# Four graph-attention layers: normalised rows transposed by DMA, and a changed opening

## The chip, the cores and the metric

The kernel runs on one core of one Trainium2 chip. The metric is the device time of one execution in microseconds (us), lower being better; the number given for a kernel is the median of several executions.

## The reference

The input is `x` with 16 batches of 1024 nodes and 256 features, and an adjacency matrix of 1024 x 1024. Four layers follow each other, each with a residual connection:

```python
h = jnp.maximum(_layernorm(x, axis=-1), 0.0)
x = x + layer(h, adj, W, a)
```

A layer projects the rows (`Wh = h @ W`), forms for each pair of nodes i, j a score `leaky_relu(e_src[i] + e_dst[j])`, masks it by the adjacency matrix, takes the softmax over j, sums the projected rows with these weights and applies elu (the last layer: relu). Layers 0 and 2 have four heads of 64 features, layers 1 and 3 one head of 256.

## The kernel before, in words

One step is one layer of one batch; there are 64 steps. Four batches (streams) are in work at a time, and `order_of_steps` interleaves them so that, from step 7 to step 58, four-head and one-head steps alternate. At the start three four-head steps follow each other, and near the end (steps 59 and 60) two.

The 1024 nodes lie as 8 chunks of 128 partitions. The work of a step falls into three parts.

**Preparation** (`preparation(n)`) is a list of 21 small pieces: row statistics of each half (four chunks) on VectorE (DVE, L238), their combination on GpSimd (POOL), `normalise` on ScalarE (ACT, L283), `transpose` on TensorE (PE, L291) with an eviction that applies relu (L292), `project` for each chunk on PE (L302) with its eviction to `whx` (L304), two exponentials (L310, L312), a scaling on POOL (L314), `factors`, and `rows`, which transposes the small matrix of factors (L326), copies it (L328), writes it to DRAM as `grow` (L330) and so makes it possible to fetch it back as rows. For each head `fetch` reads one row of `grow` into all partitions (`gs`, L344, on the SP queue), and `broadcast` copies it to PSUM as `g` (L350, ACT).

**Weights and aggregation.** For each head and each chunk of source nodes, `weights` makes one tile `w` of 128 x 1024 on DVE (L355). `aggregate` multiplies these with `whx` on PE (L371), in eight groups per step: in a four-head step two groups per head, each over four chunks of target nodes; in a one-head step one group per chunk. ACT copies each result out of PSUM to `y` (L386). A head's eight `w` tiles are used by all its groups, and come free after the last one. The ring of `w` tiles has `WBUFS = 18` buffers. PSUM banks for PE's results are a ring of four.

**Finish** (`finish(n)`), during the next step: reciprocal (L403), scaling (L413 on DVE or L416 on POOL, L414 on POOL), exponential (L420), and the additions for elu and residual (L426, L427; L429 in the last layer).

The order is written by hand. Each kind of step has a table (`FOUR`, `SHORT`, `ONE`, `SOON`, `FIRST`, `TIGHT`, `LATE`) with 21 due times, one per piece of the preparation in the order: two statistics, combination, two normalisations, two transposes of the first half, four projections, two transposes of the second half, four projections, factors, rows, fetch, end. The unit is a group, the zero is the start of step n - 2, and eight units are a step. After the aggregation of group k of step n the kernel emits all pieces that are due by 8 n + k. The first step's pieces are ordered by a list of their own, `order`, between the pieces that build the two masks (`sign`, `turn` on PE, `positive` on DVE L211, `nonzero`, the squares, on ACT L215). Every engine works through its instructions in the order in which they were emitted, and so does SP with its transfers.

Of the kernel before, what the change touches and what calls it, by code (L numbers as in the profile page):

```python
# [26 lines left out]
F32 = mybir.dt.float32  # L27
BF16 = mybir.dt.bfloat16
I32 = mybir.dt.int32
U8 = mybir.dt.uint8  # L30
AF = mybir.ActivationFunctionType
ALU = mybir.AluOpType
AX = mybir.AxisListType
# [2 lines left out]
P = 128  # L36
EPS = 1e-5
SHIFT = 60.0
STREAMS = 4
WBUFS = 18  # L40

# [1 line left out]

FOUR = (-8, -8, -5, -3, -2, -1, -1, 0, 0, 0, 0, 0, 0, 2, 2, 2, 2, 3, 8, 8, 10)
SHORT = (-4, -4, -4, -2, -2, -1, -1, 0, 0, 0, 0, 0, 0, 2, 2, 2, 2, 3, 8, 8, 10)
ONE = (2, 2, 2, 4, 4, 5, 5, 6, 6, 6, 6, 6, 6, 8, 8, 8, 8, 8, 10, 10, 12)  # L50
SOON = (0, 0, 0, 1, 2, 3, 3, 4, 4, 5, 5, 5, 5, 6, 6, 7, 7, 8, 9, 9, 11)
FIRST = (-4, -4, -4, -2, 0, -1, -1, -1, -1, -1, -1, 1, 1, 2, 2, 2, 2, 2, 3, 3, 5)
TIGHT = (5, 5, 5, 7, 7, 8, 8, 9, 9, 9, 9, 9, 9, 10, 10, 10, 10, 10, 11, 11, 13)
LATE = (0, 0, 0, 1, 1, 2, 2, 3, 3, 3, 3, 3, 3, 4, 4, 4, 4, 5, 6, 6, 8)


LAYERS = [
    (4, 0.2, 0, 0),
    (1, 0.2, 0, 0),
    (4, 0.2, 128, 1),  # L60
    (1, 0.01, 0, 1),
]
# [3 lines left out]
def kernel(ctx: ExitStack, tc: tile.TileContext, x, adj, ws, avs, out):  # L66
    nc = tc.nc
    B, N, F = x.shape
    C = N // P
    K = F // P  # L70
# [155 lines left out]
    def preparation(n):  # L226
# [50 lines left out]
            engine.tensor_scalar(shift, shift, -0.5, None, op0=ALU.mult)  # L277

        def normalise(half):
            xn = st["xn", half] = prep.tile([P, HALF, F], F32, name="xn")  # L280
            for q in range(HALF):
                c = half * HALF + q
                nc.scalar.activation(xn[:, q, :], xs[b][:, c, :], AF.Identity,  # L283
                                     bias=st["shift"][:, c:c + 1], scale=st["rstd"][:, c:c + 1])

        def transpose(half, k):
            if k == 0:
                st["hT", half] = prep.tile([P, K, HALF * P], F32, name="hT")
            pt = bank(HALF, P)
            for q in range(HALF):  # L290
                nc.tensor.transpose(pt[:, q, :], st["xn", half][:, q, k * P:(k + 1) * P], ident)  # L291
            nc.scalar.activation(st["hT", half][:, k, :], pt.rearrange("p q i -> p (q i)"),  # L292
                                 AF.Relu)

        def project(c):
            if c == 0:
# [43 lines left out]

    def fetch(n, h):

        gs = state[n]["gs", h] = work.tile([P, N], F32, name="gs", bufs=2)
        nc.sync.dma_start(out=gs, in_=state[n]["grow"][h].rearrange("c i -> (c i)")  # L344
                          .partition_broadcast(P))

    def broadcast(n, h):

        g = state[n]["g", h] = ps_g.tile([P, N], F32, name="g")
        nc.scalar.activation(g, state[n]["gs", h], AF.Copy)  # L350

    def weights(n, h, jc):
# [6 lines left out]
    def aggregate(n, h, i0, per):  # L359
# [25 lines left out]
            return  # L385
        nc.scalar.activation(st["y"][:, i0:i0 + per, h, :], acc, AF.Copy)  # L386

    def finish(n):

        b, l = steps[n]  # L390
        H = LAYERS[l][0]
        D = F // H
        st = state[n]

        def views(half):
            s = slice(half * HALF, (half + 1) * HALF)
            return (xs[b][:, s, :].rearrange("p c (h d) -> p (c h) d", h=H),
                    st["y"][:, s, :, 0:D].rearrange("p c h d -> p (c h) d"),
                    st["r"][:, s, :].rearrange("p c h -> p (c h)"))

        def divide():
            st["r"] = small.tile([P, C, H], F32, name="r")
            nc.vector.reciprocal(st["r"], st["y"][:, :, :, D])  # L403

        def scaled(half):
            xh, yh, r = views(half)
            rb = r[:, :, None].to_broadcast([P, HALF * H, D])
            time = LAYERS[steps[n + 1][1]][0] == 1
            if l < L - 1:

                e = st["e", half] = prep.tile([P, HALF * H, D], F32, name="e")
                if time:
                    nc.vector.scalar_tensor_tensor(e, yh, 0.0, rb, op0=ALU.min, op1=ALU.mult)  # L413
            nc.gpsimd.tensor_tensor(yh, yh, rb, op=ALU.mult)  # L414
            if l < L - 1 and not time:
                nc.gpsimd.tensor_scalar(e, yh, 0.0, -3.0e38, op0=ALU.min, op1=ALU.max)  # L416

        def exponential(half):
            if l < L - 1:
                nc.scalar.activation(st["e", half], st["e", half], AF.Exp)  # L420

        def add(half):
            xh, yh, r = views(half)
            if l < L - 1:
                e = st["e", half]
                nc.vector.scalar_tensor_tensor(e, e, -1.0, yh, op0=ALU.add, op1=ALU.max)  # L426
                nc.gpsimd.tensor_add(xh, xh, e)  # L427
                return
            nc.vector.scalar_tensor_tensor(xh, yh, 0.0, xh, op0=ALU.max, op1=ALU.add)  # L429

        def store(half):
            nc.sync.dma_start(
                out=out[b].rearrange("(p c) f -> p c f", p=P)[:, half * HALF:(half + 1) * HALF],
                in_=xs[b][:, half * HALF:(half + 1) * HALF, :])
            if half == 1 and b + STREAMS < B:
                load(b + STREAMS)


        at = (0, 0, 0, 0, 1, 1, 1) if H > 1 else (0, 0, 1, 1, 2, 2, 3)
        return list(zip(at, (divide, lambda: scaled(0), lambda: scaled(1), lambda: exponential(0),  # L440
                             lambda: exponential(1), lambda: add(0), lambda: add(1)))) + (
                    [(4, lambda: store(0)), (4, lambda: store(1))] if l == L - 1 else [])
# [15 lines left out]
    def prepare(upto):  # L458

        while agenda and agenda[0][0] <= upto:  # L460
            _, n, piece, last = agenda.pop(0)
            piece()
            if last:
                done["prepared"] = n + 1
# [16 lines left out]
    def emit_heads(i):  # L481

        while done["g"] <= min(i + C // 2, done["tiles"] + C, len(tiles) - 1):
            n, h, _ = tiles[done["g"]]
            if n >= done["prepared"]:
                break
            broadcast(n, h)
            done["g"] += C
            fetch_heads()

    def emit_tiles(upto, must=False):
        while done["tiles"] < min(upto, len(tiles)):
            i = done["tiles"]
            if i == done["g"] and tiles[i][0] >= done["prepared"] and must:
                prepare(max(a[0] for a in agenda if a[1] == tiles[i][0]))
            emit_heads(i)
            if i >= done["g"]:
                return
            weights(*tiles[i])
            done["tiles"] += 1  # L500

    last, agenda_of = {}, []
    for n, (b, l) in enumerate(steps):

        free = 8 * (last[b % STREAMS] + 1) + (8 if l == 0 else 2) if b % STREAMS in last else -99
        last[b % STREAMS] = n
        start = 8 * (n - 2) + (n == 3)
        kind = (ONE if n < len(steps) - 2 else TIGHT) if LAYERS[l][0] == 1 else SOON if n < 5 else FOUR
        if kind is FOUR and free > start + kind[0]:
            kind = SHORT  # L510
        if free > start + kind[0]:
            kind = LATE
            start = max(free, agenda_of[-1][0] + 5, start - LATE[7])
        agenda_of.append([start + k for k in kind] if n > 1 else FIRST)
        if n > 2:

            assert agenda_of[n][7] >= 8 * (n - 2)
            was = agenda_of[n - 1]
            assert agenda_of[n][3] >= was[5] and agenda_of[n][4] >= was[11]
    ending = []  # L520
    later = {}
    with tc.manual_schedule():
# [9 lines left out]
        for i in range(2, STREAMS):  # L532
# [10 lines left out]

            + [blocks[c][1] for c in range(4)]
            + [first[7], first[8], blocks[0][2], blocks[4][1], blocks[5][1], blocks[0][3],
               first[9], first[10], blocks[1][2], blocks[0][4], blocks[6][1], blocks[7][1],
               blocks[1][3], first[11], first[12], blocks[2][2], blocks[1][4],
               lambda: prepare(-4), first[13], first[14], blocks[3][2], blocks[2][4],
               blocks[2][3], blocks[3][3], first[15], first[16]]

            + [first[17], blocks[4][2], blocks[5][2], first[18], first[19],
               blocks[4][3], blocks[3][4], blocks[4][4], blocks[5][3], blocks[5][4],
               blocks[6][2], blocks[7][2], blocks[6][3], blocks[6][4], blocks[7][3], blocks[7][4]])
        plan(1)
        planned = 2
        for piece in order:
            piece()
        done["prepared"] = 1
        emit_tiles(C // 2, must=True)
        prepare(-2)  # L560
        emit_tiles(C, must=True)
        prepare(-1)
        for i in range(2, STREAMS):
            load_weights(i)

# [59 lines left out]
```

## Time and profile before

| | |
|---|---|
| median of 10 runs | 2562.13 us (2559.81 to 2564.59) |
| the profiled execution | 2562.18 us, of which the span is 2560.4 us |
| mean granted TensorE clock | 0.992 |
| PE busy | 2495.2 us, 97% of the span |
| DVE busy | 2019.2 us, 79% |
| ACT busy | 1130.7 us, 44% |
| POOL busy | 1112.2 us, 43% |
| DMA | 129.01 MB moved, queue q1 13.7% of 16 engines' time |

The span runs from the first to the last instruction. Busy times of PE count matmuls as overlapping stretches; PEld is the loading of the stationary operand, which overlaps with them. In a group's row the columns are the busy time, the mean duration of one instruction in ns, and the idle time of its engine just before them with what ended it.

### The profile page before, as it was taken

Reading aid. Unit: us, or ns where it says so; the run is one execution under the profiler, and the core shown is the slowest. Engines: PE = TensorE matmul, PEld = TensorE weight load, DVE = VectorE, ACT = ScalarE, POOL = GpSimd, SP = SyncE. Lnnn points to the kernel's source line nnn. Section 1 sums busy time; section 2 is a strip of 40 time slices with the busy share of each in tenths; the row PEclk is TensorE's granted clock in tenths of the full one; section 3 lists DMA queues with packets and bytes.
Section 4 is the critical chain, followed back from the end, with each engine's and each line's share of the span. In section 5 each row is a group of like instructions: output and inputs, shape, how many; then the busy total and the mean of one; then the engine's idle time right before and its main releaser. Section 6 shows DMA issues by size and latency. Waiting matters only on the chain.

```text
span 2560.4 us, 88174 instructions
## 1 busy us (share of the span) xinstructions
PE 2495.2 (97%) x40088; PEld 2256.7 (88%) x40088; DVE 2019.2 (79%) x2140; ACT 1130.7 (44%) x2502; POOL 1112.2 (43%) x1364
## 2 busy tenths in 40 slices
PE   6889999999999999999999999999999999999899
PEld 5788889999988999988899889999888899898887
DVE  8888577888778888778888778878778878778863
ACT  5344454434444444544434544444444444544331
POOL 3244455533444544544333544543443444644341
PEclk8999999999999999999999999999999999999999
DMA  5101011121211110111221111111112210111101
GB/s 182 53 27 43 10 43 35 44 77 47 73 43 68 44 44 11 43 43 68 77 75 45 43 35 44 43 41 46 72 40 76 76 36 19 43 35 43 61 10 58
DMA packets 36991, 129.01 MB, mean 50 GB/s; under 512 B 6278, under 2 KB 9094, under 8 KB 34696
## 3 DMA queue, kind: packets, MB, share of 16 engines
q1 hardware_dynamic: 36606, 123.36, 13.7%
q8 instruction: 314, 5.14, 0.8%
q14 instruction: 61, 0.50, 0.1%
q10 hardware_dynamic: 10, 0.00, 0.0%
HBM read 105.91 MB, written 17.43 MB: 48 GB/s over the span
## 4 chain that ended last, share of the span: by engine, by line
PE 88%; DVE 6%; ACT 3%; issue 2%; POOL 1%; DMA 0%; DVEq 0%; POOLq 0%; ACTq 0%
PE bank L371 68%; PE bank L302 15%; DVE w L355 5%; PE bank L291 4%; ACT xn L283 2%; DVE bn L238 0%; PE bank L326 0%; POOL y L414 0%; POOL e L416 0%; ACT g L350 0%; ACT y L386 0%; POOL shift L277 0%; DVE e L426 0%; DMA x<-in_x 0%; DMA gs<-grow 0%
## 5 line engine op out<-in xcount | busy, mean ns | idle before, releaser
L371 PE MATMUL bank<-whx,w 128*64 128x65 f32 x36864 | 1908.5, 241 | 30.9 <-DVE w L355 17.5
L371 PEld LDWEIGHTS bank<-whx,w 128*64 128x64 f32 x36864 | 1744.0, 145 | 175.8 <-DVE w L355 24.1
L355 DVE SCALAR_TENSOR_TENSOR w<-g,rcol,mask 128x1024 f32<-128x1024 f32 x1280 | 1540.3, 1273 | 392.1 <-PE bank L371 316.0
L386 ACT ACTIVATE y<-bank 128x260 f32<-128x260 f32 (+1 forms) x504 | 194.3, 385 | 1091.5 <-PE bank L371 1091.5
L414 POOL TENSOR_TENSOR y<-y,r 128x1024 f32<-128x1024 f32 x126 | 263.6, 2102 | 580.2 <-DVE e L413 448.8
L314 POOL TENSOR_TENSOR whx<-whx 128x1024 f32<-128x1024 f32 x128 | 257.8, 2014 | 581.7 <-ACT whx L312 581.7
L302 PE MATMUL bank<-wx,hT 128*128 128x264 f32 (+1 forms) x2048 | 482.1, 388 | 6.4 <-ACT y L386 4.3
L302 PEld LDWEIGHTS bank<-wx,hT 128*128 128x128 f32 x2048 | 382.5, 191 | 77.2 <-ACT y L386 15.5
L427 POOL TENSOR_TENSOR x<-x,e 128x1024 f32<-128x1024 f32 x96 | 248.0, 2594 | 136.4 <-DVE e L426 135.3
L283 ACT ACTIVATE xn<-x,shift,rstd 128x256 f32<-128x256 f32 x512 | 264.7, 590 | 73.1 <-POOL shift L277 70.6
L304 ACT ACTIVATE whx<-bank 128x264 f32<-128x264 f32 (+1 forms) x512 | 189.2, 385 | 177.9 <-PE bank L302 177.6
L238 DVE BATCH_NORM_STATS2 bn<-x 128x6 f32<-128x256 f32 x512 | 175.9, 411 | 79.6 <-POOL x L427 76.3
L426 DVE SCALAR_TENSOR_TENSOR e<-e,y 128x1024 f32<-128x1024 f32 x96 | 154.2, 1625 | 37.5 <-ACT e L420 30.3
L350 ACT ACTIVATE g<-gs 128x1024 f32<-128x1024 f32 x160 | 163.5, 1022 | 11.4 <-DVE w L355 9.7
L291 PE MATMUL bank<-ident,xn 128*128 128x128 f32 x1024 | 137.0, 276 | 10.4 <-ACT xn L283 10.2
L291 PEld LDWEIGHTS bank<-ident,xn 128*128 128x128 f32 x1024 | 120.1, 142 | 27.6 <-ACT xn L283 14.5
L292 ACT ACTIVATE hT<-bank 128x512 f32<-128x512 f32 x256 | 136.9, 586 | 1.3 <-PE bank L291 1.0
L271 POOL TENSOR_TENSOR rstd<-rstd,neghalf 128x4 f32<-128x4 f32 (+1 forms) x97 | 120.4, 1241 | 15.1 <-DVE shift L272 7.7
L420 ACT ACTIVATE e<-e 128x1024 f32<-128x1024 f32 x96 | 100.7, 1049 | 24.2 <-POOL e L416 23.8
L413 DVE SCALAR_TENSOR_TENSOR e<-y,r 128x1024 f32<-128x1024 f32 x60 | 72.5, 1250 | 2.2
L429 DVE SCALAR_TENSOR_TENSOR x<-y,x 128x1024 f32<-128x1024 f32 x30 | 44.9, 1499 | 2.0 <-POOL y L414 2.0
L265 POOL TENSOR_TENSOR dev<-bn 128x4 f32<-128x4 f32 (+1 forms) x95 | 20.7, 217 | 49.3 <-DVE bn L238 49.2
(63 smaller groups left out, 463.4 us busy)
## 6 DMA issues: line engine op xcount, KB each, us to landing
gs<-grow SPq DMA_DIRECT2D x160, 512.0 KB
x<-in_x SPq DMA_DIRECT2D x15, 1024.0 KB
out<-x SPq DMA_DIRECT2D x30, 512.0 KB
w<-in_adj SPq DMA_DIRECT2D x8, 512.0 KB
x<-in_x SPq DMA_DIRECT2D x2, 512.0 KB
wx<-in_L_gnn_W SPq DMA_DIRECT2D x8, 128.0 KB
out<-x SPq DMA_DIRECT2D x8, 128.0 KB
grow<-gT SPq DMA_DIRECT2D x32, 16.0 KB
```

The source lines that it names most:

```text
L238: nc.vector.bn_stats(bn[:, c, :], xs[b][:, c, :])
L283: nc.scalar.activation(xn[:, q, :], xs[b][:, c, :], AF.Identity, bias=st["shift"][:, c:c + 1], scale=st["rstd"][:, c:c + 1])
L291: nc.tensor.transpose(pt[:, q, :], st["xn", half][:, q, k * P:(k + 1) * P], ident)
L302: nc.tensor.matmul(pw, lhsT=st["hT", half][:, k, q * P:(q + 1) * P], rhs=wx[l][:, k, :], start=(k == 0), stop=(k == K - 1))
L304: nc.scalar.activation(st["whx"][:, c, :], pw, AF.Copy)
L314: nc.gpsimd.tensor_tensor(wh[:, :, :, 0:D], wh[:, :, :, 0:D], wh[:, :, :, D:D + 1].to_broadcast([P, HALF, H, D]), op=ALU.mult)
L350: nc.scalar.activation(g, state[n]["gs", h], AF.Copy)
L355: nc.vector.scalar_tensor_tensor(w, state[n]["g", h], state[n]["rcol"][:, jc, h:h + 1], masks[LAYERS[steps[n][1]][3]][:, jc, :], op0=ALU.m ...
L371: nc.tensor.matmul(acc[o % P:o % P + cols, q, :], lhsT=st["w", h, jc][:, o:o + cols], rhs=st["whx"][:, jc, h * (D + 1):(h + 1) * (D + 1)], ...
L386: nc.scalar.activation(st["y"][:, i0:i0 + per, h, :], acc, AF.Copy)
L414: nc.gpsimd.tensor_tensor(yh, yh, rb, op=ALU.mult)
L427: nc.gpsimd.tensor_add(xh, xh, e)
```

## The change

The core of the diff, in two parts. The first part alters the opening. For head 0 of step 0, `fetch` does nothing and `broadcast` makes `g` by eight PE transposes of the factors, each with a column spread over 128:

```diff
     def broadcast(n, h):
         g = state[n]["g", h] = ps_g.tile([P, N], F32, name="g")
+        if n == 0 and h == 0:
+            for c in range(C):
+                nc.tensor.transpose(g[:, c * P:(c + 1) * P],
+                                    state[n]["gcol"][:, c, h:h + 1].to_broadcast([P, P]), ident)
+            return
         nc.scalar.activation(g, state[n]["gs", h], AF.Copy)
```

The list `order` changes, the squares of a pair of masks standing behind both of the pair's `positive`. In `finish`, a four-head step that is followed by another four-head step spreads its pieces over groups 0 to 3; the scaling on DVE (L413) now needs four heads and a following one-head step:

```diff
+    def slack(n):
+        return LAYERS[steps[n + 1][1]][0] == 1
...
-            time = LAYERS[steps[n + 1][1]][0] == 1
...
-                if time:
+                if H > 1 and slack(n):
...
-        at = (0, 0, 0, 0, 1, 1, 1) if H > 1 else (0, 0, 1, 1, 2, 2, 3)
+        at = (0, 0, 0, 0, 1, 1, 1) if slack(n) and H > 1 else (0, 0, 1, 1, 2, 2, 3)
```

The second part concerns the transposes. From step 2 on, PE's transposes and their evictions are replaced. `normalise` applies the relu and writes its result with the two halves of the features outermost. `split` copies it on ACT as 16-bit integers, all lower halves of the words ahead of all upper halves; a transposing DMA from the SP queue turns each of the 16 blocks of 128 x 128; `merge` puts the halves together again on ACT. The two pieces of `transpose` are now `split` and `merge`:

```diff
+        def split(half):
+            xn = st["xn", half].rearrange("p k q i -> p (k q i)").bitcast(U16)
+            bits = prep.tile([P, 2, K * HALF * P], U16, name="rows", bufs=HBUFS)
+            nc.scalar.activation(bits, xn.rearrange("p (n s) -> p s n", s=2), AF.Copy)
+            st["turned", half] = prep.tile([P, 2, K * HALF, P], U16, name="rows", bufs=HBUFS)
+            nc.sync.dma_start_transpose(
+                out=st["turned", half].rearrange("p s n i -> p (s n) i"),
+                in_=bits.rearrange("p s n -> p (s n)"))
+
+        def merge(half):
+            st["hT", half] = prep.tile([P, K, HALF * P], F32, name="rows", bufs=HBUFS)
+            nc.scalar.activation(
+                st["hT", half].rearrange("p k i -> p (k i)").bitcast(U16).rearrange(
+                    "p (n s) -> p n s", s=2),
+                st["turned", half].rearrange("p s n i -> p (n i) s"), AF.Copy)
+
         def transpose(half, k):
+            if n > 1:
+                (merge if k else split)(half)
+                return
```

The buffers of `xn`, `hT` and the new tiles become one ring `rows` of `HBUFS = 5`, and `WBUFS` goes from 18 to 17. The tables get new due times; the two that the alternating steps use are

```diff
-FOUR = (-8, -8, -5, -3, -2, -1, -1, 0, 0, 0, 0, 0, 0, 2, 2, 2, 2, 3, 8, 8, 10)
+FOUR = (-8, -8, -5, 0, 2, 1, 4, 5, 5, 5, 5, 3, 4.5, 5, 5, 5, 5, 6, 8, 8, 10)
-ONE = (2, 2, 2, 4, 4, 5, 5, 6, 6, 6, 6, 6, 6, 8, 8, 8, 8, 8, 10, 10, 12)
+ONE = (2, 2, 2, 3, 4, 3, 5, 7, 7, 7, 7, 4, 7, 8, 8, 8, 8, 8, 11, 11, 12)
```

## The prediction

> **What bounds the kernel now.** I read the page from the top: busy shares first, then the chain that ended last, then the costliest groups.
>
> ```profile
> span 2560.4 us, 88174 instructions
> ...
> PE 2495.2 (97%) x40088; PEld 2256.7 (88%) x40088; DVE 2019.2 (79%) x2140; ACT 1130.7 (44%) x2502; POOL 1112.2 (43%) x1364
> ...
> PE 88%; DVE 6%; ACT 3%; issue 2%; POOL 1%; DMA 0%; DVEq 0%; POOLq 0%; ACTq 0%
> PE bank L371 68%; PE bank L302 15%; DVE w L355 5%; PE bank L291 4%; ACT xn L283 2%; DVE bn L238 0%; PE bank L326 0%; POOL y L414 0%; POOL e L416 0%; ACT g L350 0%; ACT y L386 0%; POOL shift L277 0%; DVE e L426 0%; DMA x<-in_x 0%; DMA gs<-grow 0%
> ...
> L355 DVE SCALAR_TENSOR_TENSOR w<-g,rcol,mask 128x1024 f32<-128x1024 f32 x1280 | 1540.3, 1273 | 392.1 <-PE bank L371 316.0
> ...
> L350 ACT ACTIVATE g<-gs 128x1024 f32<-128x1024 f32 x160 | 163.5, 1022 | 11.4 <-DVE w L355 9.7
> L291 PE MATMUL bank<-ident,xn 128*128 128x128 f32 x1024 | 137.0, 276 | 10.4 <-ACT xn L283 10.2
> ...
> L292 ACT ACTIVATE hT<-bank 128x512 f32<-128x512 f32 x256 | 136.9, 586 | 1.3 <-PE bank L291 1.0
> ```
>
> TensorE is busy 97% and carries 88% of the chain; 4% is L291, the transposes that the change takes away. DVE comes second and waits for PE (316 us): its w tiles are made ahead until the 18 buffers are full. Those buffers are the only cushion, so I asked the windows for one pair of steps in the middle (a four-head step at 1051.19, then a one-head step) and for the opening.
>
> ```profile
> 1051.19:1127.96 76.77, 76.68 (x1252) 69.72 (x1254) 61.49 (x65) 35.84 (x80) 38.50 (x45) 1.00 0.12 37
> ...
> 45.80:200.50 154.70, 136.94 (x3249) 126.36 (x3249) 134.17 (x138) 62.23 (x133) 50.88 (x63) 0.93 0.10 34
> ```
>
> Columns: length, then busy PE, PEld, DVE, ACT, POOL, clock, DMA share, GB/s. In the pair PE has no hole (76.68 of 76.77) and DVE has 15 us to spare. In the opening, three four-head steps in a row, PE has 18 us of holes: there DVE paces. The timeline of the pair gives the unit prices:
>
> ```profile
> 1051.12 3.95 PE L371 MATMUL bank<-whx,w 128*64 128x65 f32 x128
> 1055.00 7.31 PE L302 MATMUL bank<-wx,hT 128*128 128x258 f32 x32
> 1062.15 1.04 PE L291 MATMUL bank<-ident,xn 128*128 128x128 f32 x8
> 1063.12 7.69 PE L371 MATMUL bank<-whx,w 128*64 128x65 f32 x256
> ```
>
> and DVE's own timeline of the same stretch:
>
> ```profile
> 1066.30 7.24 DVE L355 SCALAR_TENSOR_TENSOR w<-g,rcol,mask 128x1024 f32<-128x1024 f32 x6 [9.29 <-PE bank L371]
> ```
>
> From start to start, eight transposes cost 0.97 us of PE, eight projections 7.2 (0.9 each), a group of a four-head step 3.75 to 3.88; a w tile is 1.2 us of DVE. The 9.29 us in brackets is DVE waiting until PE has used up head 0.
>
> **What the Trainium skill says.** "ScalarE: Activation LUTs", section "What ACT_TABLE_LOAD costs": an activation costs a fixed part and 0.833 ns per element, float32 or bf16 alike. The trace agrees on float32, (1022 - 385) / (1024 - 260) = 0.834 ns between L350 and L386; no run here shows 16-bit elements two apart. "VectorE: DVE Perf Modes", section "The three transpose paths": 390 ns for a 128x128 bf16 transpose on TensorE and 1309 ns by the DMA crossbar. In the trace one float32 transpose is 272 ns recorded but 0.12 us in a run of eight; no DMA transpose is in it. "DMA: Bandwidth & Descriptors", section "Latency and other measured facts": 261 GB/s for DMA transposes. "Advanced Engine Details and Errata", section "X-Bar Transpose (TRN2)": they are about as fast as plain ones, and only one stream may transpose at a time; here SP alone issues them.
>
> **The change part by part**
>
> *Transposes of steps 2 to 63.* 62 steps x 2 halves = 124 halves, each with eight PE transposes: 124 x 0.98 us = 121.5 us leave PE. Steps 2, 3 and 4 are prepared in the opening, where DVE paces: 3 x 1.96 = 5.9 us bring nothing. Counted: -115.6 us.
>
> *ACT.* Per half two evictions L292 go (2 x 0.586 = 1.17 us); a split and a merge of 2048 elements come, each 1.022 + 1024 x 0.000834 = 1.88 us. So +2.58 us per half, 124 x 2.58 = +320 us: ACT goes from 1131 to about 1450 us, 59% of the new span, not a bound. Relu moves into the normalisation at no cost. Behind a split or merge wait the evictions of y and whx, and PE waits for those when its four banks are full; a group lasts 3.5 to 3.75 us, so a bank is free for over 10 us in aggregation, and a delay of 1.9 us is covered there. In a burst of projections (0.9 us each) the cover is only some 3 us: zero taken, up to +15 us kept for the range.
>
> *The DMA.* Each half sends 128 x 2048 x 2 bytes = 0.5 MB on SP's queue. The nearest row is the gs fetch of the same size: 3.92 us from issue to arrival (32.60 to 36.52 on the chain). By the skill's bandwidth, an estimate of 524288 / 261000 = 2.0 us of transfer, with the roughly 1.7 us that the gs fetch has beside its 2.2 us of issue spacing (four of them in 8.84 us in the pair's timeline): 3.7 us. By the skill's 1309 ns per block, sixteen blocks end to end: 20.9 us. I take 5 us. SP's instruction waits for the split; behind it on SP stand the gs fetches, x loads and stores, whose rows are needed a head or more later. The added 62 MB is half of what q1 moves in 13.7% of the engines' time, so about 7% more.
>
> *Is 5 us hidden?* In a four-head step the second half is split after group 3 and merged after group 5. After group 3's end ACT takes y (0.39) and the split (1.88), so the transfer has 2 x 3.75 - 2.27 = 5.2 us before ACT itself must wait. PE has four projections of the first half (3.6 us) before it needs the merge (1.88): 5.2 + 3.6 - 1.9 = 6.9 us. In a one-head step (groups of 3.47 us) the same working, with normalisation and split in one group and a first transfer before the second, also gives about 7. So 5 us cost nothing and each us beyond 7 costs PE about 1 us per step.
>
> *Projections bunched, 17 buffers.* FOUR now puts all eight projections at group 5; before, four stood at group 0 and four at group 2 of that step, and gave DVE time. So: head 0 is used up at 3.75 + 3.65 (the one-head step's four projections) + 3.75 = 11.2 us. With 17 buffers DVE has then made 16 tiles and one of head 2; seven more (8.4 us) and an elu add between (1.24) end at 20.8. PE is through head 1 at 18.7 and can use seven tiles, to 19.5. **A new wait of 1.3 us** in each of about 28 such steps: +36 us. Afterwards the eight projections (7.2 us) restore DVE's lead. Bounds: 0 (a longer group gives the time back) and 2.5 us per step, one tile more late.
>
> *The first G.* grow, gs and the copy go; eight PE transposes (1.0 us) take their place. Before, gcol is ready at 30.06, G at 37.56, and DVE ends its masks at 34.49; now masks bound: 37.60 - 34.49 = -3.1 us. The other order of first pieces, squares behind masks, prepares in the opening, and the elu spread over groups 0 to 3 where four heads follow four act on the 18 us of holes there; not priced by any row, so bounded by 0 and -15; I take -9. Together -12.
>
> Sum: -115.6 + 36 - 12 = -92 us against the profiled execution's 2562.18 (span 2560.4 and 1.8 around it), which equals the median, 2562.13. **Forecast 2470 us.**
>
> **Rivals**
>
> *Part of the gain is eaten* (2500 to 2556): the wait on w is 2.5 us per step (+34 more), or the transfer takes 7.5 us (31 us more), or ACT's burst costs its 15. For it: DVE falls from 15 to 11 us of slack per pair. Against it: the lead is regained each step.
>
> *The transfer lands late* (slower): from 7 us on, each us costs 62 us; the 92 us gained are gone at 7 + 1.5 = 8.5 us. At 10 us the time is 2470 + 3 x 62 = 2656. For it: 1309 ns per block in sequence gives 20.9, transfers of two halves queue behind each other and behind the gs fetches. Against it: the DMA engines are 12% busy, and both bandwidth figures lie far below the point. If 16-bit elements cost ACT two beats, split and merge gain 1.7 us each and eat the same window; with 5 us that ends near zero gain.
>
> *It does not do what it says*: steps 0 and 1 keep PE transposes (32 records); all others must go.
>
> **How the numbers follow.** Forecast case 0.50, by its bounds 2430 to 2500. Eaten gain 0.27. Within 0.2%, about what a measurement tells from no change, 0.04. Slower 0.19, nearly all by late landing. The range goes from 2430 (0.04 below: no wait on w and all of the opening) to 2570 (0.17 above). The likeliest sign's own range is 2430 to 2556.
>
> **What would show it.** L291 down to 32 transposes on PE; PE near 2375 us; a pair near 74.2 us (76.8 - 3.9 + 1.3); PE idle before L371 by DVE w, about 1.3 us in each four-head step; split and merge at 1.88 us; a DMA transpose under 7 us; L302 waiting for a merge nowhere. I am wrong if ACT waits long for the transposing DMA and PE's idle is put down to that, or if DVE's w waits vanish.

## The result, and the profile after

| | before | after |
|---|---|---|
| median | 2562.18 us (29 runs) | 2478.91 us (8 runs, 2476.93 to 2482.28) |
| ratio, with its 95% interval | | 0.9678 (0.9669 to 0.9686) |
| the profiled execution, and its span | 2562.18 us, 2560.4 | 2482.28 us, 2480.5 |

The change makes the kernel 83.3 us faster; 92 were forecast. These are the lines of the page after it: busy shares, queue q1, the chain that ended last, and the costliest groups. The lines have moved: L283, L291, L302, L304, L355, L371, L386 and L350 are now L285 (normalise), L316 (the transposes left on PE), L327 (project), L329 (eviction to `whx`), L388 (`w`), L404 (aggregate), L419 (eviction to `y`) and L383 (copy of `g`). New are L294 (split), L296 (the transposing DMA) and L302 (merge).

```profile
span 2480.5 us, 86492 instructions
...
PE 2404.1 (97%) x39104; PEld 2156.7 (87%) x39104; DVE 2044.5 (82%) x2138; ACT 1481.5 (60%) x2501; POOL 1073.0 (43%) x1366
...
q1 hardware_dynamic: 294382, 187.86, 30.4%
...
PE 87%; DVE 6%; DMA 3%; ACT 2%; issue 2%; POOL 1%; DVEq 0%; SPq 0%; ACTq 0%; POOLq 0%
...
L388 DVE SCALAR_TENSOR_TENSOR w<-g,rcol,mask 128x1024 f32<-128x1024 f32 x1280 | 1540.6, 1272 | 230.7 <-PE bank L404 134.4
...
L302 ACT ACTIVATE rows<-rows 128x2048 uint16<-128x2048 uint16 x124 | 265.7, 2143 | 15.8 <-DMA rows<-rows 15.8
L294 ACT ACTIVATE rows<-rows 128x2048 uint16<-128x2048 uint16 x124 | 236.2, 1904 | 2.2
...
rows<-rows SPq DMA_TRANSPOSE x124
```

PE is still the bound, and 91 of its busy microseconds are gone. ACT has 351 more. DVE waits for PE 134 us where it waited 316: its lead in `w` tiles has shrunk. In the windows, the pair of steps that is shown and the opening answer to those of before (length, busy PE, PEld, DVE, ACT, POOL, clock, DMA share, GB/s):

```profile
1019.30:1093.50 74.20, 73.97 (x1219) 66.37 (x1218) 63.17 (x65) 47.11 (x79) 36.68 (x44) 1.00 0.28 66
943.97:1019.30 75.33, 73.83 (x1219) 66.51 (x1218) 63.09 (x65) 47.10 (x79) 36.69 (x44) 1.00 0.30 65
45.30:185.40 140.10, 128.36 (x3201) 117.73 (x3201) 133.90 (x139) 77.02 (x130) 49.38 (x63) 0.95 0.26 64
```

One pair takes 74.20 us, and the pair ahead of it 75.33 with the same work: a pause came in. The four stretches of the program, by the starts of their first aggregations, add up to the difference of the two spans:

| | before | after | difference |
|---|---|---|---|
| start of step 0 to start of step 3, and the 0.5 us ahead of it | 154.7 | 140.1 | -15.1 |
| step 3 to step 7 | 157.7 | 155.1 | -2.7 |
| 25 pairs, steps 7 to 56 | 1926.9 | 1875.8 | -51.1 (-2.04 a pair) |
| from step 57 to the end | 275.3 | 264.3 | -11.0 |

**Where 3.92 us per pair became 2.04.** The idle stretches between PE's weight loads that are over 0.2 us, summed over the 25 pairs and divided by 25, give this list:

| PE waits | before | after |
|---|---|---|
| for `w` of head 2 (four-head step) | 0 | 0.36 |
| inside a group of the four-head step (after: always group 5), for nothing that the profile shows | 0.16 | 0.66 |
| inside the eight projections, for the eviction to `whx` | 0 | 0.36 |
| for the merge, end of the one-head step | 0 | 0.34 |
| inside the one-head step's projections, for the eviction to `y` | 0.59 | 0 |
| hand-over from a run of projections to the aggregation behind it | 0.34 | 1.01 |
| other | 0 | 0.04 |
| sum | 1.09 | 2.78 |

The transposes of a pair's four halves were 3.92 us of PE's work. So 3.92 - 1.69 = 2.23 is to be had, and 2.04 is there. The same sum for e15, below, gives 2.48 where 2.72 came: the list is good to some 0.2 us. PE's timeline of the pair at 1019.30 shows the first row, the wait for `w` in front of the second part of head 2's first group (start, duration, then the idle time and what ended it):

```profile
1038.46 1.04 PE L404 MATMUL bank<-whx,w 128*64 128x65 f32 x28
1039.72 6.87 PE L404 MATMUL bank<-whx,w 128*64 128x65 f32 x228 [0.22 <-DVE w L388]
1046.52 7.67 PE L327 MATMUL bank<-wx,rows 128*128 128x264 f32 x32
```

It falls where the prediction put it, at the eighth tile of head 2, in all 25 pairs. It is much shorter than the 1.3 us forecast.

The second row, in the pair at 943.97:

```profile
964.33 6.28 PE L404 MATMUL bank<-whx,w 128*64 128x65 f32 x207 [0.22 <-DVE w L388]
...
971.88 0.81 PE L404 MATMUL bank<-whx,w 128*64 128x65 f32 x21 [1.27 <-issue]
```

"issue" says that no semaphore explains it. There are 12 such pauses in the 25 pairs (16.5 us; 7 with 3.9 us before). All 12 end 2.2 to 2.7 us after the start of a 16 KB packet of the queue that brings instructions (q8), and the 7 of the kernel before end 2.2 to 2.9 us after one. My reading is that PE has run out of instructions and goes on when that packet has come. That the transposing transfers delay it is less sure. Packets of such a transfer run during each of the 12 pauses (in the one shown SP had issued it at 965.69). But the kernel before and e15 (5 pauses, 2.5 us) have none of these transfers, in 6 of e2's 17 pauses none is under way, and e6 with twice as many has only two pauses.

The third row is the chain of a late merge. SP's, ACT's and PE's timelines of one pair, in that order:

```profile
889.86 0.33 SPq L371 DMA_DIRECT2D gs<-grow  x1
890.25 4.45 SPq L296 DMA_TRANSPOSE rows<-rows  x1
```

```profile
898.31 2.15 ACT L302 ACTIVATE rows<-rows 128x2048 uint16<-128x2048 uint16 x1 [1.99 <-DMA rows<-rows]
```

```profile
895.81 3.83 PE L327 MATMUL bank<-wx,rows 128*128 128x264 f32 x16
900.78 3.83 PE L327 MATMUL bank<-wx,rows 128*128 128x264 f32 x16 [1.14 <-ACT whx L329]
```

SP issues the transpose right behind a `gs` fetch of the same size. The transfer's last packet ends 6.0 us after the issue, where 3.8 us is the median of all 124, and the merge starts 8.1 us after the issue. ACT, which works in order, stands 1.99 us in front of the merge; the evictions behind it come late; and PE, with four banks full, stands 1.14 us in the middle of its projections.

### The profile page after: what moved, and what is told of

Its sections match the earlier page's. It is cut to its first block, busy times and chain, and to the rows that moved or that the text cites. A ratio compares the mean times of both kernels' runs of the same rounds, so it can differ in the third digit from the quotient of the medians.

```text
span 2480.5 us, 86492 instructions
## 1 busy us (share of the span) xinstructions
PE 2404.1 (97%) x39104; PEld 2156.7 (87%) x39104; DVE 2044.5 (82%) x2138; ACT 1481.5 (60%) x2501; POOL 1073.0 (43%) x1366
## 3 DMA queue, kind: packets, MB, share of 16 engines
q1 hardware_dynamic: 294382, 187.86, 30.4%
## 4 chain that ended last, share of the span: by engine, by line
PE 87%; DVE 6%; DMA 3%; ACT 2%; issue 2%; POOL 1%; DVEq 0%; SPq 0%; ACTq 0%; POOLq 0%
PE bank L404 69%; PE bank L327 18%; DVE w L388 4%; DMA rows<-rows 2%; ACT rows L302 1%; DVE bn L240 1%; ACT rows L285 0%; DVE e L462 0%; ACT rows L294 0%; DVE mask L213 0%; POOL x L463 0%; DMA x<-in_x 0%; PE bank L351 0%; POOL rstd L273 0%; DVE wx L160 0%
## 5 line engine op out<-in xcount | busy, mean ns | idle before, releaser
L404 PE MATMUL bank<-whx,w 128*64 128x65 f32 x36864 | 1908.5, 241 | 43.3 <-DVE w L388 26.7
L404 PEld LDWEIGHTS bank<-whx,w 128*64 128x64 f32 x36864 | 1753.7, 145 | 204.6 <-DVE w L388 32.6
L388 DVE SCALAR_TENSOR_TENSOR w<-g,rcol,mask 128x1024 f32<-128x1024 f32 x1280 | 1540.6, 1272 | 230.7 <-PE bank L404 134.4
L339 POOL TENSOR_TENSOR whx<-whx 128x1024 f32<-128x1024 f32 x128 | 243.6, 1903 | 857.5 <-ACT whx L337 857.5
L419 ACT ACTIVATE y<-bank 128x260 f32<-128x260 f32 (+1 forms) x504 | 191.8, 384 | 664.2 <-PE bank L404 663.7
L327 PE MATMUL bank<-wx,rows 128*128 128x264 f32 (+1 forms) x2048 | 487.9, 392 | 12.2 <-ACT rows L302 6.2
L327 PEld LDWEIGHTS bank<-wx,rows 128*128 128x128 f32 x2048 | 383.2, 192 | 88.3 <-ACT rows L302 14.4
L463 POOL TENSOR_TENSOR x<-x,e 128x1024 f32<-128x1024 f32 x96 | 227.0, 2365 | 179.0 <-DVE e L462 179.0
L285 ACT ACTIVATE rows<-x,shift,rstd 128x256 f32<-128x256 f32 x512 | 264.5, 589 | 66.6 <-POOL shift L279 64.3
L329 ACT ACTIVATE whx<-bank 128x264 f32<-128x264 f32 (+1 forms) x512 | 189.5, 386 | 170.8 <-PE bank L327 170.4
L302 ACT ACTIVATE rows<-rows 128x2048 uint16<-128x2048 uint16 x124 | 265.7, 2143 | 15.8 <-DMA rows<-rows 15.8
L294 ACT ACTIVATE rows<-rows 128x2048 uint16<-128x2048 uint16 x124 | 236.2, 1904 | 2.2
L462 DVE SCALAR_TENSOR_TENSOR e<-e,y 128x1024 f32<-128x1024 f32 x96 | 191.2, 1992 | 48.9 <-ACT e L456 38.0
L240 DVE BATCH_NORM_STATS2 bn<-x 128x6 f32<-128x256 f32 x512 | 175.5, 410 | 33.3 <-POOL x L463 30.0
L383 ACT ACTIVATE g<-gs 128x1024 f32<-128x1024 f32 x159 | 162.6, 1023 | 27.7 <-DVE w L388 15.0
L273 POOL TENSOR_TENSOR rstd<-rstd,neghalf 128x4 f32<-128x4 f32 (+1 forms) x97 | 120.4, 1241 | 15.1 <-DVE shift L274 7.7
L440 DVE RECIPROCAL r<-y 128x32 f32<-128x32 f32 (+1 forms) x63 | 17.3, 274 | 86.3 <-ACT y L419 86.3
L337 ACT ACTIVATE whx<-whx,nbias 128x16 f32<-128x16 f32 (+1 forms) x128 | 40.3, 315 | 4.2
```

The source lines that it names most:

```text
L240: nc.vector.bn_stats(bn[:, c, :], xs[b][:, c, :])
L285: nc.scalar.activation(xn[:, :, q, :], xs[b][:, c, :].rearrange("p (k i) -> p k i", k=K), AF.Relu, bias=st["shift"][:, c:c + 1], scale=st[ ...
L294: nc.scalar.activation(bits, xn.rearrange("p (n s) -> p s n", s=2), AF.Copy)
L302: nc.scalar.activation(st["hT", half].rearrange("p k i -> p (k i)").bitcast(U16).rearrange("p (n s) -> p n s", s=2), st["turned", half].re ...
L327: nc.tensor.matmul(pw, lhsT=st["hT", half][:, k, q * P:(q + 1) * P], rhs=wx[l][:, k, :], start=(k == 0), stop=(k == K - 1))
L339: nc.gpsimd.tensor_tensor(wh[:, :, :, 0:D], wh[:, :, :, 0:D], wh[:, :, :, D:D + 1].to_broadcast([P, HALF, H, D]), op=ALU.mult)
```

## The experiments

My theory is the prediction's: PE's time is its work plus its holes; the transposes' work is gone, and what comes back are waits at places that the order of the pieces sets, the ring of `w` among them. Theory A of each run is what this gives for it, and the rival B is told with the run. Ratios are to the kernel before, on the same chip.

**e1: PE transposes put back, all else as changed.**

```diff
-            if n > 1:
+            if n > len(steps):
                 (merge if k else split)(half)
```

> The changed kernel with the transposes of steps 2 to 63 back on TensorE, at the places of split and merge; opening, tables and 17 buffers of w as changed. Theory A (the gain is PE time taken away, part of it given back as waits for w and for late merges): PE gets 121.5 us back, the 2 us per pair of waits that the trace of the changed kernel shows go away (25 x 2 = 50), so about 2479 + 121 - 50 = 2550 us, PE busy some 80 us more, no wait of L327 for a merge. Rival B (the gain is mostly the opening and the new due times): 2500 us or less.

2875.64 us, ratio 1.1229 (1.1212 to 1.1246). Both missed by over 300 us. The new due times let normalisation and the first transpose fall into one group, which is right for a split on ACT and wrong for PE, which then waits in order for the normalised rows (waits: engine and line, releaser, us in total, times, longest):

```profile
PEld bank L316 <- ACT rows L285: 274.8, 280, 8.3
```

In the kernel after, this row has 10.6 us. So due times and the place of the transpose belong together, and undoing one alone does not price the other. The fair comparison is e15.

**e2: one `w` buffer fewer.**

```diff
-WBUFS = 17
+WBUFS = 16
```

> The changed kernel with 16 buffers of w instead of 17. Theory A (at head 2 of a four-head step PE waits for the tile that could not be made ahead): one tile more is late, 1.2 us in each of 28 steps, +34 us, 2513; the wait shows as L404 <- DVE w L388, and a pair is 76.2 us. Rival B (that wait is covered by the merge's wait behind it, which ends last in the same head): at most +10 us.

2512.24 us, ratio 0.9807 (0.9791 to 0.9823): 33.3 us above the changed kernel's median, as theory A had it (2513). Over some 28 four-head steps that is 1.19 us a step, near the 1.27 us of one `w` tile, and the wait is the one named:

```profile
PEld bank L404 <- DVE w L388: 68.1, 73, 3.6
```

against 32.6 us in 42 times in the kernel after. With 17 the ring of `w` tiles is at its limit: one buffer less is paid in full.

**e4: the first part of the change, with the new due times for the first five steps.** The opening's edits are in, the DMA is not; steps 5 and later keep the old tables, and the ring of `w` has its 18 buffers.

```diff
-            if n > 1:
+            if n > len(steps):
                 (merge if k else split)(half)
...
+        if n >= 5:
+            kind = (OLD_ONE if n < len(steps) - 2 else OLD_TIGHT) if LAYERS[l][0] == 1 else OLD_FOUR
```

> The opening of the change alone: first G by TensorE, order of first pieces, due times of steps 1 to 4, elu over more groups where four heads follow four; from step 5 on the due times of before, 18 buffers of w, transposes on TensorE everywhere. Theory A: the 15.1 us by which step 3 starts earlier in the changed kernel's trace (185.4 against 200.5) stay to the end, 2562 - 15 = 2547 us. Rival B: VectorE's lead is used up either way in steps 4 to 7 and less than 5 us stay, 2557 us or more.

2564.06 us, ratio 1.0011 (1.0003 to 1.0018). The number is near B's, the reason isn't: step 3 starts at 213.2 us, 12.7 later than before, since `SOON` too lets PE's transposes stand behind a normalisation of the same group (PE's weight loads wait 24.9 us for the normalised rows by then). This is e1's fault again, so the run doesn't price the opening; e14 does.

**e5: the first G by DMA again, all else as changed.**

```diff
     def fetch(n, h):
-        if n == 0 and h == 0:
-            return
...
     def broadcast(n, h):
-        if n == 0 and h == 0:
-            for c in range(C):
-                nc.tensor.transpose(g[:, c * P:(c + 1) * P],
-                                    state[n]["gcol"][:, c, h:h + 1].to_broadcast([P, P]), ident)
-            return
```

> The changed kernel with the first head's G fetched through DRAM and copied by ScalarE as before, everything else as changed. Prediction's step: +3.1 us (2482). What the trace shows: VectorE's first w starts at 36.29 instead of 37.60, so +1.3 us in the opening (2480), as the masks end at 36.2 and bound it. Rival: ScalarE's squares now stand ahead of the copy of G, so that it comes later than in the kernel before, +4 us or more.

2482.66 us, ratio 0.9687 (0.9672 to 0.9701), not to be told from the changed kernel's 0.9678 (0.9669 to 0.9686). In the traces DVE's first `w` starts 7.6 us after the factors are ready here (30.19 to 37.83), 7.5 in the kernel before (30.06 to 37.60) and 5.3 in the kernel after (30.95 to 36.29). DVE's timeline has a wait for G here, and none in the kernel after (first line: here, second: after; L380 and L375 are here what L388 and L383 are there):

```profile
37.83 9.63 DVE L380 SCALAR_TENSOR_TENSOR w<-g,rcol,mask 128x1024 f32<-128x1024 f32 x8 [3.29 <-ACT g L375]
...
36.29 9.62 DVE L388 SCALAR_TENSOR_TENSOR w<-g,rcol,mask 128x1024 f32<-128x1024 f32 x8
```

So the first G by PE is worth about 2.3 us at that place. It is not more because its eight transposes stand on PE ahead of those of the last masks: the masks end 5.2 us after the factors (36.18), where they end 4.4 us after them here (34.54), and they bind next.

**e6: every transposing transfer made twice.**

```diff
-            nc.sync.dma_start_transpose(
-                out=st["turned", half].rearrange("p s n i -> p (s n) i"),
-                in_=bits.rearrange("p s n -> p (s n)"))
+            for _ in range(2):
+                nc.sync.dma_start_transpose(
+                    out=st["turned", half].rearrange("p s n i -> p (s n) i"),
+                    in_=bits.rearrange("p s n -> p (s n)"))
```

> The changed kernel with each transposing transfer sent twice (the same data to the same place), so that the merge waits for both. In the changed kernel's trace a transfer's packets end 3.8 us after its issue, 5 to 6.7 us where a gs fetch was issued just before. Theory A (hidden up to about 7 us, then one us of PE per us and step): the pairs' later halves land at 8 to 10 us, some 2 us too late in a four-head step and 1 in a one-head step, +60 to +100 us, so 2540 to 2580. Rival B (the window is wider, ACT and the four banks cover it): under +20 us. Rival C (transfers hold up the engines' other traffic): over +150 us, with gs fetches late and L383 waiting for DMA.

2946.56 us, ratio 1.1502 (1.1483 to 1.1521): far beyond A and B. The size is C's, but the way is not: ACT waits 58.1 us for the `gs` rows (12.7 in the kernel after) and six times as long for the transposed ones. The two transfers of a half follow each other (two occupy SP for 8.27 us where one took 1.5 to 4.8), and ACT stands in front of the merge:

```profile
ACT rows L303 <- DMA rows<-rows: 343.0, 84, 8.1
```

The time is 468 us above that of the kernel after. Per pair PE has 7.1 us of holes behind late evictions and 4.9 in front of merges, some 300 us in the 25 pairs, and beyond that the mean granted clock is 0.928 against 0.991. In group 5 of the four-head steps the merges of both halves now start 10.2 us after the first issue, in the median; for 10 us the prediction's late-landing rival had 2656 us. It was thus a real danger and was priced too gently.

**e7: in four-head steps, the second half's merge and projections later.**

```diff
-FOUR = (-8, -8, -5, 0, 2, 1, 4, 5, 5, 5, 5, 3, 4.5, 5, 5, 5, 5, 6, 8, 8, 10)
+FOUR = (-8, -8, -5, 0, 2, 1, 4, 5, 5, 5, 5, 3, 6, 6, 6, 6, 6, 6, 8, 8, 10)
```

`SHORT` has the same edit, here and in e10, e12 and e13.

> In FOUR and SHORT the second merge and its four projections due one group later (6 instead of 4.5 and 5). Theory A (the eight projections ahead of head 3 are what gives VectorE time for head 3's tiles): the late merge's wait at group 5 goes (about -1.2 us per pair), but PE reaches head 3 3.7 us earlier than VectorE can follow: +1 to +2.5 us per pair net, 2500 to 2540. Rival B (only the late merge costs): -1.2 x 28 = -34 us, 2445.

2584.6 us, ratio 1.0080 (1.0065 to 1.0095), 106 us above the kernel after; both missed. In the kernel after, the merge is emitted in group 5 with the four projections of the first half between it and its own. Here merge and projections stand alone in group 6, behind that group's eviction to `y`, and PE reaches the projections before the merge has run. PE's timeline has two runs of four projections (16 matmuls each), one without and one behind that hole:

```profile
921.37 3.83 PE L327 MATMUL bank<-wx,rows 128*128 128x264 f32 x16
925.13 3.95 PE L404 MATMUL bank<-whx,w 128*64 128x65 f32 x128
931.60 5.51 PE L327 MATMUL bank<-wx,rows 128*128 128x264 f32 x16 [2.52 <-ACT rows L302]
```

and the windows over the first run, the hole, and the second run:

```profile
921.30:925.10 3.80, 3.80 (x22) 2.96 (x16) 3.80 (x4) 1.56 (x4) 0.00 (x0) 1.00 0.00 0
929.00:931.60 2.60, 0.08 (x5) 0.00 (x1) 2.60 (x3) 2.42 (x2) 0.00 (x0) 1.00 0.00 0
931.60:937.00 5.40, 5.40 (x16) 4.07 (x16) 3.14 (x3) 1.17 (x3) 0.00 (x0) 0.68 0.01 3
```

After the hole the granted clock is 0.68 and the same four projections take 1.7 us longer, so that a hole of 2.5 us costs 4.2. This is so in 14 of the 25 pairs (5.3 to 5.5 us). In the other 11 the hole is as long, and the projections behind it take 3.83 us, as in the next pair:

```profile
1012.27 3.83 PE L327 MATMUL bank<-wx,rows 128*128 128x264 f32 x16 [2.51 <-ACT rows L302]
```

**e8: in one-head steps, the second half's merge and projections later.**

```diff
-ONE = (2, 2, 2, 3, 4, 3, 5, 7, 7, 7, 7, 4, 7, 8, 8, 8, 8, 8, 11, 11, 12)
+ONE = (2, 2, 2, 3, 4, 3, 5, 7, 7, 7, 7, 4, 8, 10, 10, 10, 10, 10, 11, 11, 12)
```

> In ONE the second merge due at 8 and its four projections and the factors at 10, that is after group 2 of the four-head step instead of after group 0. Theory A (head 0 is used up 3.7 us earlier, so VectorE can make head 2's tiles in time, and the merge at the end of the one-head step has more time): the wait for w at head 2 (0.4 us) and the 0.4 us at group 7 of the one-head step go, -0.6 to -0.8 us per pair, 2455 to 2463. Rival B: the lead is lost again at head 2's second group, no change within 5 us.

2467.68 us, ratio 0.9628 (0.9612 to 0.9644): 11 us below the kernel after, in the direction of A and short of its 2455 to 2463. Four projections (3.65 us of PE) now stand behind group 2 of the four-head step instead of group 0. Head 0 is used up that much earlier, and DVE gains the time: the eighth tile of head 2 is done 2.6 us before PE begins with that head, where it was done 1.2 us after that in the kernel after. The wait for `w` at head 2 is gone, which shows that the order of the pieces made it. Part of it comes back at the eviction behind the late merge, 0.76 us a pair for 0.36.

**e10: in four-head steps, the second split ahead of the `gs` fetch.**

```diff
-FOUR = (-8, -8, -5, 0, 2, 1, 4, 5, 5, 5, 5, 3, 4.5, 5, 5, 5, 5, 6, 8, 8, 10)
+FOUR = (-8, -8, -5, 0, 2, 1, 4, 5, 5, 5, 5, 2.9, 4.5, 5, 5, 5, 5, 6, 8, 8, 10)
```

> In FOUR and SHORT the second split due at 2.9 instead of 3: it is emitted in the same group, but ahead of the one-head step's grow and gs, so that the transposing transfer stands ahead of the gs fetch on SP. Theory A (the second merge is late because its transfer lies behind the gs fetch): it lands in 3.8 us instead of 5 to 6.7, the wait at group 5 goes, -0.9 to -1.2 us per pair, 2445 to 2455. Rival B (the fetch that now stands behind it is itself needed): ACT waits for gs at its next copy, and the time stays or grows, 2479 to 2530.

2591.15 us, ratio 1.0107 (1.0087 to 1.0127). B's mechanism, larger than B had it. The merge's wait for its transfer does shrink, as A had it (ACT: 3.9 us in all for 15.8). But the transpose waits on SP for its split, the fetch stands behind it, and ACT waits for the fetch:

```profile
ACT g L383 <- DMA gs<-grow: 119.4, 29, 6.2
```

The kernel after has 12.7 us there. One of the two transfers has to be second, and the merge is the one with the more cover.

**e12: in four-head steps, merge behind the first four projections, the other four a group later.**

```diff
-FOUR = (-8, -8, -5, 0, 2, 1, 4, 5, 5, 5, 5, 3, 4.5, 5, 5, 5, 5, 6, 8, 8, 10)
+FOUR = (-8, -8, -5, 0, 2, 1, 4, 5, 5, 5, 5, 3, 5, 6, 6, 6, 6, 6, 8, 8, 10)
```

> The changed kernel with, in FOUR and SHORT, the second merge due at 5 behind the first four projections instead of at 4.5 ahead of them, and the second four projections and the factors due at 6. So the merge runs on ACT while PE works on group 6, and no projection stands behind it in the same group. Theory A (what cost in e7 was the merge standing in the same group as its projections, 2.5 us of wait and a slower PE after it; and what costs in the changed kernel at group 5 are projections kept up by a merge that waits for its transfer): the 1.2 us per pair at group 5 go, -25 to -33 us, 2446 to 2454. Rival B (VectorE can no longer follow at head 3 when four of the eight projections come behind it): waits for w at head 3 instead, 2479 to 2500.

2481.81 us, ratio 0.9692 (0.9679 to 0.9705): no difference from the kernel after. The wait for the eviction (0.36 a pair) is gone as A said; but the projections are now two runs, and the second hand-over to the aggregation costs 0.34. B's waits for `w` at head 3 didn't come. What is gained at one place is lost at a place that neither theory had.

**e13: e12 and e8 together.** Both diffs of e12 and e8.

> e12 and e8 together: in ONE too the second half's merge is due at 8 and its projections and factors at 10. Theory A: both gains add, about 2467 - 29 = 2438 us, PE nearly without a hole in the pairs, a pair about 73.2 us. Rival B: spread this far, VectorE is late at head 2 or 3 of the four-head step, as PE meets it with fewer projections between: 2460 or more.

2457.09 us, ratio 0.9598 (0.9585 to 0.9611): 21.8 us below the kernel after, the best of all. The interval lies below that of the kernel after and of e8. A's 2438 was too low. Its page, and a pair of its steps in the windows:

```profile
PE 2398.5 (98%) x39104; PEld 2151.5 (88%) x39104; DVE 2051.8 (84%) x2138; ACT 1484.4 (61%) x2501; POOL 1086.5 (44%) x1366
```

```profile
854.80:928.60 73.80, 73.80 (x1221) 66.38 (x1220) 63.16 (x65) 47.13 (x79) 37.58 (x44) 1.00 0.28 66
```

PE has no wait for `w` in the pairs; left are pauses for instructions (8, 0.36 us a pair), the merge at the end of the one-head step (0.36) and four hand-overs of 0.33.

**e14: the first part of the change alone, with every due time of before.**

```diff
+        if n == 0 and h == 0:
+            for c in range(C):
+                nc.tensor.transpose(g[:, c * P:(c + 1) * P],
+                                    state[n]["gcol"][:, c, h:h + 1].to_broadcast([P, P]), ident)
+            return
...
-        at = (0, 0, 0, 0, 1, 1, 1) if H > 1 else (0, 0, 1, 1, 2, 2, 3)
+        at = (0, 0, 0, 0, 1, 1, 1) if slack(n) and H > 1 else (0, 0, 1, 1, 2, 2, 3)
...
-               first[9], first[10], blocks[1][2], blocks[0][4], blocks[6][1], blocks[7][1],
+               first[9], first[10], blocks[1][2], blocks[6][1], blocks[7][1], blocks[1][3],
...
```

> The kernel before with the opening's pieces alone (first G by TensorE, the other order of first pieces with the squares behind both masks, elu over more groups) and every due time, 18 buffers and PE transposes as before. Theory A, after e4 (the due times of steps 1 to 4 fit only the DMA transposes, the pieces themselves bring a little): -5 to -9 us, 2553 to 2557, step 3 starts some 3 us earlier than 200.5 and the two four-head steps near the end are about 5 us shorter. Rival B: the whole -15 us of the opening belong to these pieces: 2547 or less.

2543.3 us, ratio 0.9933 (0.9919 to 0.9946), -18.0 us and nearer to B. Step 3 starts at 192.8 us instead of 200.5, and step 60, near the end, where four heads follow four, takes 36.7 us instead of 44.6. So the first part's gain has two places: 7.7 us in the opening and 7.9 in step 60, which the prediction didn't look at. In the kernel after, step 60 takes 43.2 us: together with the second part most of this gain is gone, and why isn't shown.

**e15: the second part's gain with nothing in its place.** The kernel before, without transposes and their evictions from step 2 on; the projections read the rows untransposed, so that the results are not those of the layer. Besides what the diff shows, the relu moves into the normalisation, and `xn` and `hT` share a ring of four buffers.

```diff
         def transpose(half, k):
+            if n > 1:
+                st["hT", half] = st["xn", half].rearrange("p q f -> p (q f)").rearrange(
+                    "p (k i) -> p k i", k=K)
+                return
```

> The kernel before with the transposes of steps 2 to 63 and their evictions left out: the projections read the normalised rows untransposed, in tiles of the same shape; all else as before, 18 buffers of w. It measures what the PE time is worth with nothing put in its place. Theory A (PE sets the pace, and VectorE's lead of 0.6 to 1.3 us at head 3 and at the one-head step is used up before the whole 121.5 us are): 3.9 us per pair less work, about 1 us of it turned into waits for w, -85 to -100 us, 2462 to 2477. Rival B: VectorE takes over fully, under -60 us. Rival C: all 121.5 us, 2440.

2478.64 us, ratio 0.9682 (0.9669 to 0.9695): -82.7 us, short of A. A pair takes 74.35 us, 2.7 less than before and not 3.9. What the eight transposes had covered comes out in PE's timeline:

```profile
939.79 1.14 PE L306 MATMUL bank<-wx,xn 128*128 128x258 f32 x4 [0.91 <-ACT y L390]
```

The projections of the one-head step run into evictions that have not been done yet, 1.41 us a pair for 0.59 before. Two hand-overs into an aggregation, 0.35 and 0.33 us a pair, are new as well, at places where transposes had stood; waits for `w`, which A had expected, are not. So even taking the work away for nothing yields 82.7 of the 121.5 us that the work takes, and in the pairs these waits, which the transposes had covered, are enough to explain the 1.2 us that do not come.

## Why the prediction was right, step by step

**Sign, size and main mechanism held.** L316 keeps the 32 transposes of steps 0 and 1, and 2478.91 us is 0.4% from 2470. But the terms did not hold one by one.

- *Transposes, -115.6.* The work went as counted: 3.92 us a pair. That its worth equals its length was wrong: e15 brings 82.7 us with nothing put in its place. PE's busy time fell by 91 us and not by the 120 that the forecast of 2375 takes. Busy time hides part of the loss: the pair at 1019.30 shows 73.97 busy of 74.20, with several of the listed waits in it.
- *Wait for `w`, +36.* Right in place, cause and steps (e2, e8); 0.36 us and not 1.3. PE came to head 2 about 0.4 us later than worked out (19.1 us for 18.7), and head 0 was used up about 0.4 us earlier (10.8 for 11.2): together 0.8 of about 1 us. Some 10 us came where 36 stood.
- *ACT at no cost.* Nearly right in the sum, wrong in its parts. New are 0.36 us a pair inside the projections and 0.34 in front of the merge; against them stand 0.59 for `y` that went. The net is 0.11 us a pair, 3 us in all. "L302 waiting for a merge nowhere" failed (the projection is L327 now): its weight loads waited for the merge 28 times, 14.4 us. The price was 1.88 us for split and merge alike; the split took 1.90 and the merge 2.14. The Trainium skill, "ScalarE: Activation LUTs", section "What ACT_TABLE_LOAD costs", has one price per element for every function, float32 and bf16 alike. The split, which reads every second 16-bit element, agrees; the merge, which reads by turns from two stretches 1024 elements apart, took 0.26 us more. ACT's total rose by 351 us instead of 320.
- *The DMA, 5 us, hidden.* The last packet of a transfer ends 3.8 us after its issue (median), and 4.7 to 7.0 us after it in the 28 that were issued within 1 us behind a `gs` fetch. So of the two estimates, 3.7 and 20.9 us, the first was near, and the 5 us taken were too little mainly behind a fetch. ACT waited over 0.3 us in front of 17 merges (15.8 us in all), where it had come 4.2 to 6.8 us after the issue, 6.2 in the median; 5.2 had been worked out. PE's own limit was near the 6.9 us worked out: in the four-head steps it did not wait behind the merge that began 6.84 us after the issue. Its weight loads waited behind the 12 that began 6.85 to 7.34 us after it, 0.2 to 0.8 us behind nine and 1.1 to 2.1 behind three, and 1.56 us behind the one at 8.06.
- *"Each us beyond 7 costs PE about 1 us per step".* Most of the waits just named fit this roughly. With every transfer late (e6) the term was too small, since the merges of both halves are late in one group and hold up the evictions behind them, and since holes can lower the clock (e6, e7).
- *The opening, -12.* It was -15.1 to step 3. The first G was worth about 2.3 us and not 3.1: the prediction let the masks end where they had, and G's own transposes put them off. The edits of the opening bring 7.7 us with the old due times (e14). The other 7.4 come from the missing transposes and the new due times together; so the 5.9 us of steps 2 to 4 that were written off as worthless may well have counted. In e15, which has neither the new opening nor the new due times, step 3 starts at 197.2 us, 3.3 earlier than before. That is a hint and no more: in the kernel after, e7, e10 and e12, whose openings are the same, step 3 starts between 181.9 and 185.4 us.
- *Not in the sum at all:* pauses of PE for no releaser, +0.50 us a pair against before, and hand-overs from projections to aggregation, +0.67. The two are two thirds of the holes that the change added. The hand-overs come with the transposes' going, since e15 has as much of them without the DMA (+0.68). The two are the main reason why 2.04 us a pair came and not 2.62, though the wait for `w` had been priced at nearly four times what it took.

The two misses, the wait that was priced too high and the holes that were not in the sum, cancel in part, and that the forecast lies 9 us off owes something to this. Open are whether the transfers make the pauses longer, and the split of the opening's 7.4 us.

## What to carry to other kernels

Work taken off the bound engine was worth its length minus what it covered: e15 got 82.7 of 121.5 us for free removal, so ask for each removed instruction which eviction or tile was being finished beside it. When a step moves to another engine, its due times must move with it, and a piece that runs on another engine needs enough other work between it and its consumer; here the same operations ran in 2457 us (e13) or in 2585 (e7) depending on the due times alone. A ring that feeds the bound engine can be given time without another buffer, by moving other work of that engine to where the ring's tiles come free earlier (e8, e13).

## What the runs showed of the hardware that I had not expected

- **A hole of 2.5 us can cost clock.** In the pair of e7 that is shown the granted clock was 0.68 over the next 5.4 us, and four projections took 5.51 us for 3.83. The Trainium skill, "TensorE: Matmul & The Clock Gate", section "Why this matters for your kernels", asks for no gaps over about 3 us; here 2.5 us were enough, in 14 of 25 cases. What decides between equal holes is open.
- **The last packet is not the release.** In ten of the 17 waiting merges 2.05 to 2.10 us passed from the end of the transfer's last packet to the start of the merge, in the other seven 0.5 to 1.4; in the pair shown it was 6.0 and 8.1 us after the issue, with ACT idle for 1.99. A landing time read off the packets was too early by that.
- **A transpose is many small packets.** The 124 transfers are 2048 packets of 256 bytes each; q1's share of the engines' time went from 13.7% to 30.4% for about half as many bytes again, where the prediction had said 7% more.
